# One ViT layer on one core: the lanes of the low waves change from wave-then-row to row-then-wave

## The chip, the core and the metric

The kernel runs on one core of a Trainium2 chip. A core has five engines with queues of their own: TensorE (PE, with weight loads shown apart as PEld), VectorE (DVE), ScalarE (ACT), GpSimd (POOL) and SyncE (SP), and 16 DMA engines that move data between HBM and the core's 128-partition memory. The time is the device time of the whole program in microseconds (us).

## The reference, cut to what matters

The program tokenizes 16 images of 1024 patches, then does one layer of attention and a small mixture of experts. What matters here is what happens to the keys of the attention: every element `x` of the 256 x 1024 keys of an image is replaced by a Fourier sum of 256 frequencies.

```
def kan_transform(x, kan_a, kan_b):
    freqs = jnp.arange(1, NUM_FUNCTIONS + 1, dtype=x.dtype)      # 1..256
    def body(acc, fab):
        f, af, bf = fab
        return (acc + af * jnp.sin(f * x) + bf * jnp.cos(f * x), None)
    out, _ = jax.lax.scan(body, jnp.zeros_like(x), (freqs, kan_a, kan_b))
    return out
...
k = kan_transform(k, kan_a, kan_b)
dots = jnp.einsum('bhqd,bhkd->bhqk', q, k) * scale
attn = jax.nn.softmax(dots, axis=-1)
```

## The kernel before

A frequency from 1 to 256 is written as one of 16 steps 16 w + 8.5 (w from 0 to 15; the program calls these waves *low*) plus or minus one of 8 offsets v + 0.5 (*high*). By the addition theorems the sum over all frequencies of one key row becomes sines of the 16 low waves, mixed by TensorE with the coefficients, times sines of the 8 high waves, summed by TensorE.

**Where the waves come from.** `keys` computes the keys of an image as turns (the angle as a 32-bit integer) and stores them from GpSimd to a buffer in HBM, `ud`, of shape [64, 2, 4, 2, 1024]: 64 blocks of four key rows, the angle once with a quarter turn added and once without (`f`), four rows (`e`), and every row twice (`i`), 1024 tokens. A row of 1024 integers has 4 KB.

**Groups.** Eight key rows are a group; an image has 32 groups (`NG`), the 16 images have 512. A group needs three tiles `w` of 128 partitions x 1024 (512 KB each), made by `load_waves`: two for the low waves (`j` = 0 and 1, line L709, one DMA of 512 KB each) and one for the high waves (`j` = 2, line L713, two DMAs of 256 KB, each for 64 partitions). All are broadcasts: a row of `ud` lands in many partitions, and each partition is then one (row, wave) pair. There are 12 buffers for `w` (`NW`).

**What is done with a tile `w`.** `turn_waves` (L728, GpSimd) multiplies it in place by the wave number of each partition, taken from the constant `lane`, so that the integers wrap round to the angle wanted. `sines` (L740, ScalarE) takes the sine. `mix` (L746, TensorE) multiplies the two low tiles by the coefficients `coef` into the PSUM tile `kan`; a column of `coef` sums over the partitions of one row. `times_fast` (L756, VectorE) multiplies `kan` by the high tile into `prod`, and `add_up` (L771, TensorE) sums that into `red`.

**Order.** The work is written out by hand in rounds: 130 rounds, of which 128 have four groups (eight low loads and four pairs of high loads). A round has four groups of waves first, then one attention step (`score` L817, `exponential` L827, `weigh` L835), and between them pieces of the other work (tokens, layer norms, queries, keys of the next image, experts), which `piece` picks by their due times. All loads of `w` go through SP's queue together with the loads of queries (`q<-qd`, L804) and keys (`k<-kd`, L792) and the stores of queries (L420) and keys (L784). GpSimd's queue holds the wave multiplications, the layer norm `hn` (L307), the stores of `ud` (L387) and the loads of the image (`x`, L286), in order.

In the kernel before, partition p of a low tile holds wave p // 8 of row p % 8: the eight rows (copy `i` = 0 of each) are written 16 times one below the other.

Of the kernel before, what the change touches and what calls it, by code (L numbers as in the profile page):

```python
# [22 lines left out]
N = 1024  # L23
# [32 lines left out]
def plain_path(ctx: ExitStack, tc: tile.TileContext, a: dict, out: bass.AP, verdict: bass.AP):  # L56
# [8 lines left out]
    nc = tc.nc  # L65
# [63 lines left out]
    for i in range(4):  # L129
        nc.sync.dma_start(out=biases[ds((NE + 1) * i, NE), 0, :], in_=a["eb3"])  # L130
        nc.sync.dma_start(
            out=biases[ds((NE + 1) * i + NE, 1), 0, :], in_=a["sb3"].unsqueeze(0)
# [13 lines left out]
    lane = const.tile([P, 2], INT, tag="lane", name="lane")  # L146
# [547 lines left out]
    def load_waves(n=NW):  # L694

        for _ in range(n):
            if ptr["load"] == min(3 * total, ptr["used"] + NW):
                return
            i = ptr["load"]
            g, j = divmod(i, 3)  # L700
            b, g = divmod(g, NG)
            st = images.get(b)
            if st is None or st.get(("rows", g // (NG // 2)), 0) < 2:
                return
            w = wp.tile([P, N], INT, tag="w", name="w")
            ud = st["ud"]
            if j < 2:
                src = ud[2 * g + j, :, :, 0, :].rearrange("f e n -> (f e) n")
                nc.sync.dma_start(out=w, in_=src.unsqueeze(0).to_broadcast([16, 8, N]))  # L709
            else:  # L710
                for s in range(2):
                    src = ud[2 * g + s].rearrange("f e i n -> (f e i) n")
                    nc.sync.dma_start(  # L713
                        out=w[ts(s, 64), :],
                        in_=src.unsqueeze(1).to_broadcast([16, 4, N]),
                    )
            w_tiles[i] = w
            ptr["load"] += 1
# [158 lines left out]
    feed(1, first_norm(0, 0), keys(0, 0))  # L877
    finish()
    load_waves()
    turn_waves(NW - 3)  # L880
    for ch in chains:
        ch["due"] = 0

    with tc.manual_schedule():
        for rd in range(B * RI + 2):
            now["round"] = rd
            b, rr = divmod(rd, RI)
# [21 lines left out]
            if attends:  # L909
                i, st = p % NPAIR, images[p // NPAIR]  # L910
# [5 lines left out]
            for n, g in enumerate(groups):  # L916
                sines(g)
                if n < 3:
                    turn_waves(1)
                if n == 0:  # L920
                    piece("sin")
                mix(g)
                if n > 0:
                    times_fast(groups[n - 1])
                    add_up(groups[n - 1])
                    if n != 2:
                        load_waves(3)
                    piece("sin")
# [3 lines left out]
            for n in range(0, NT, 2):  # L932
                if attends:
                    q4 = bands_of_queries[att]
                    score(q4, n)
                    exponential(n)
                    if n == 0:
                        piece(EXP)
                    score(q4, n + 1)
                    exponential(n + 1)  # L940
                if n == 0 and groups:
                    add_up(groups[-1])
                if n == 2 and groups and groups[-1] % 8 == 7:
                    finish_keys(groups[-1] // 8)
                if attends and n > 0:
                    weigh(p, n - 2)
                    weigh(p, n - 1)
                if n in (0, 4):
                    load_waves(3)
                if n == 2 and 0 <= att + 1 < 2 * NPAIR * B:  # L950
                    stack_queries(att + 1)
                turn_waves(2 if n < 6 else 3)
                piece(EXP)
                if n > 0 or not attends:
                    piece(EXP)
# [616 lines left out]
def _kan_layout(kan_a, kan_b):  # L1572

    a, b = kan_a.reshape(16, 16), kan_b.reshape(16, 16)
    a_hi, b_hi = a[:, 8:], b[:, 8:]
    a_lo, b_lo = a[:, 7::-1], b[:, 7::-1]
    first = np.block([[b_hi, a_hi], [a_hi, b_lo]])
    second = np.block([[b_lo, a_lo], [a_lo, b_hi]])
    outs = []
    for blk in (first, second):
        o = np.zeros((2, 32, 4, 16, 8), blk.dtype)
        for half in range(2):
            for e in range(4):  # L1590
                o[half, :, e, :, 4 * half + e] = blk
        outs.append(o.reshape(2, 128, 128))
    return outs
# [22 lines left out]
def _kan_tiles(kan_a, kan_b):  # L1616

    outs = []
    for blk in _kan_layout(kan_a, kan_b):
        b = blk[0].reshape(2, 16, 4, 2, 8, 8)[:, :, 0, :, :, 0].transpose(1, 0, 2, 3)
        o = np.zeros((16, 2, 4, 2, 4, 8), b.dtype)
        for e in range(4):
            o[:, :, e, :, e, :] = b
        outs.append(o.reshape(128, 64))
    return outs


def _waves():

    lane = np.arange(128)
    return np.stack([32 * (lane // 8) + 17, 2 * (lane % 8) + 1], 1).astype(np.int32)


def _pack():
# [63 lines left out]
```

## Time and profile before

| | |
|---|---|
| time, median of 4 runs | 5494.17 us (5474.49 to 5499.47) |
| the profiled execution: time, span | 5501.68 us, 5499.8 us |
| TensorE busy, share of the span | 4981.7 us, 91% |
| ScalarE, GpSimd, VectorE busy | 3154.2 us (57%), 3627.9 us (66%), 2382.9 us (43%) |
| granted TensorE clock, mean | 0.960 |
| bytes moved by the DMA engines | 1148.57 MB, mean 209 GB/s |
| loads of low waves (L709) | 1024 of 512 KB |
| loads of high waves (L713) | 1024 of 256 KB |

An engine's idle time costs only where it is on the path that sets the end. The profile names for each wait what ended it. The chain of the work that ended last is followed back only over the end of the program here, so the bound of the loop is read from the waits of each engine.

### The profile page before, as it was taken

Reading aid. Unit: us, or ns where it says so; the run is one execution under the profiler, and the core shown is the slowest. Engines: PE = TensorE matmul, PEld = TensorE weight load, DVE = VectorE, ACT = ScalarE, POOL = GpSimd, SP = SyncE. Lnnn points to the kernel's source line nnn. Section 1 sums busy time; section 2 is a strip of 40 time slices with the busy share of each in tenths; the row PEclk is TensorE's granted clock in tenths of the full one; section 3 lists DMA queues with packets and bytes.
Section 4 is the critical chain, followed back from the end, with each engine's and each line's share of the span. In section 5 each row is a group of like instructions: output and inputs, shape, how many; then the busy total and the mean of one; then the engine's idle time right before and its main releaser. Section 6 shows DMA issues by size and latency. Waiting matters only on the chain. (4 is left out here: it accounts for less than half of the span.)

```text
span 5499.8 us, 57562 instructions
## 1 busy us (share of the span) xinstructions
PE 4981.7 (91%) x18625; PEld 2130.0 (39%) x18625; DVE 2382.9 (43%) x3596; ACT 3154.2 (57%) x3517; POOL 3627.9 (66%) x2284
## 2 busy tenths in 40 slices
PE   6889899898999989999899998989999899998987
PEld 2324344343443434334343443434434343343334
DVE  2344435444443443444454344444434434444432
ACT  2556556555655655565565565556556555655652
POOL 6677857667576666757667576675766667576651
PEclk8999999999999999999999999999999999999998
DMA  7989988887887888888888888979879888888960
GB/s 205 225 239 221 234 214 198 224 217 208 220 221 204 209 220 214 230 204 199 220 215 229 210 199 219 216 213 220 225 201 214 212 215 231 202 199 219 217 159 14
DMA packets 360729, 1148.57 MB, mean 209 GB/s; under 512 B 53308, under 2 KB 57316, under 8 KB 352228
## 3 DMA queue, kind: packets, MB, share of 16 engines
q1 hardware_dynamic: 323044, 1010.57, 75.2%
q0 software_dynamic: 37376, 134.24, 7.4%
q8 instruction: 151, 2.47, 0.2%
q14 instruction: 158, 1.29, 0.1%
HBM read 993.61 MB, written 150.99 MB: 208 GB/s over the span
## 5 line engine op out<-in xcount | busy, mean ns | idle before, releaser
L728 POOL TENSOR_TENSOR w<-w,lane 128x1024 int32<-128x1024 int32 x1536 | 2885.8, 1908 | 1020.8 <-DMA w<-ud 798.5
L740 ACT ACTIVATE w<-w 128x1024 f32<-128x1024 int32 x1536 | 1497.7, 1046 | 327.2 <-POOL w L728 325.6
L827 ACT ACTIVATE es<-sT 128x1024 f32<-128x1024 f32 x1024 | 1036.8, 1023 | 705.4 <-PE sT L817 517.4
L746 PE MATMUL kan<-w,coef 128*64 128x512 f32 x4096 | 1191.1, 635 | 85.6 <-ACT w L740 85.5
L835 PE MATMUL av<-es,v 128*64 128x512 f32 x4096 | 1018.2, 620 | 2.1 <-DVE rc L859 2.1
L756 DVE TENSOR_TENSOR prod<-kan,w 128x1024 f32<-128x1024 f32 x512 | 626.2, 1223 | 780.3 <-PE red L771 664.9
L817 PE MATMUL sT<-q,k 128*128 128x512 f32 x2048 | 729.7, 468 | 65.3 <-ACT es L827 33.6
L771 PE MATMUL red<-prod,pack 128*64 128x512 f32 x2048 | 587.2, 632 | 208.1 <-DVE prod L756 207.5
L852 DVE RECIPROCAL rc<-av 128x512 f32<-128x512 f32 x128 | 429.5, 3356 | 781.0 <-PE av L835 780.7
L746 PEld LDWEIGHTS kan<-w,coef 128*64 128x64 f32 x4096 | 324.7, 143 | 836.6 <-issue 455.2
L827 ACT ACT_TABLE_LOAD x126 | 161.7, 1283 | 648.0 <-PE sT L817 647.9
L817 PEld LDWEIGHTS sT<-q,k 128*128 128x128 f32 x2048 | 367.3, 192 | 370.5 <-issue 162.1
L835 PEld LDWEIGHTS av<-es,v 128*64 128x64 f32 x4096 | 260.0, 140 | 515.7 <-issue 491.7
L286 POOL DMA_DIRECT2D x<-in_xT x128 | 110.6, 864 | 438.6 <-PE tok L209 303.2
L209 PE MATMUL tok<-wt,x 128*128 128x256 f32 x1536 | 377.1, 397 | 18.9 <-DMA x<-in_xT 18.9
L209 PEld LDWEIGHTS tok<-wt,x 128*128 128x128 f32 x1536 | 290.9, 196 | 159.2 <-issue 107.4
L771 PEld LDWEIGHTS red<-prod,pack 128*64 128x64 f32 x2048 | 137.0, 141 | 524.8 <-DVE prod L756 339.8
L307 POOL TENSOR_SCALAR hn<-h,mv,rstd 128x256 f32<-128x256 f32 x256 | 311.4, 1250 | 2.1 <-PE s2p L209 0.3
L209 PE MATMUL e1p<-hT,w1e 128*128 128x512 f32 x496 | 245.9, 619 | 0.9 <-ACT s L621 0.5
L346 DVE TENSOR_TENSOR h<-tok,tokb 128x256 f32<-128x256 f32 x128 | 54.1, 422 | 431.9 <-PE tok L209 431.9
L682 POOL DMA_DIRECT2D out<-h x32 | 26.5, 829 | 272.5 <-DVE h L680 228.2
L213 PE MATMUL lnT<-ident,hn 128*128 128x128 f32 x512 | 104.2, 325 | 106.8 <-POOL hn L307 102.1
(113 smaller groups left out, 4127.4 us busy)
## 6 DMA issues: line engine op xcount, KB each, us to landing
w<-ud SPq DMA_DIRECT2D x1024, 512.0 KB
w<-ud SPq DMA_DIRECT2D x1024, 256.0 KB
q<-qd SPq DMA_DIRECT2D x512, 128.0 KB
k<-kd SPq DMA_DIRECT2D x128, 512.0 KB
x<-in_xT POOLq DMA_DIRECT2D x128, 384.0 KB, 9.8
ud<-ui POOLq DMA_DIRECT2D x64, 512.0 KB, 9.9
ud<-u POOLq DMA_DIRECT2D x64, 512.0 KB, 8.2
qd<-qhi SPq DMA_DIRECT2D x64, 256.0 KB
```

What stands on the lines that cost most here:

```text
L209: nc.tensor.matmul(out=out, lhsT=lhsT, rhs=rhs, start=start, stop=stop)
L286: nc.gpsimd.dma_start(out=t, in_=xT[b, :, ts(j, XT)].rearrange("(c p) n -> p c n", p=P))
L307: nc.gpsimd.tensor_scalar(hn[:, t, :], h[:, t, :], mv[:, t, 0:1], rstd[:, t : t + 1], ALU.subtract, ALU.mult,)
L728: nc.gpsimd.tensor_tensor(w, w, f.to_broadcast([P, N]), ALU.mult)
L740: nc.scalar.activation(x, w, AF.Sin, scale=TURN * 2.0**-32)
L746: nc.tensor.matmul(out=ps[ts(j, 64), ts(blk, 512)], lhsT=coef, rhs=w_tiles[3 * g + j][:, ts(blk, 512)], start=True, stop=True,)
L756: nc.vector.tensor_mul(prod, kan.pop(g), w_tiles[3 * g + 2])
L771: nc.tensor.matmul(out=rows_of_pair[p][ts(blk, 64), :], lhsT=pack[:, ds(PACK0 - 8 * r, 64)], rhs=prod[:, ts(blk, 512)], start=(r == 0), st ...
L817: nc.tensor.matmul(out=ps[:, ts(s, 512)], lhsT=k4[:, s, ts(kc, P)], rhs=q4[:, s, :], start=True, stop=True,)
L827: nc.scalar.activation(es, scores.pop(kc), AF.Exp, scale=SCALE)
L835: nc.tensor.matmul(out=acc[0][ts(s, 64), :], lhsT=v[:, kc, p % NPAIR, ds(HD * s, 64)], rhs=es[:, ts(s, 512)], start=(kc == 0), stop=(kc == ...
L852: nc.vector.reciprocal(rc, av)
```

## The change

The low tiles' partitions are ordered by row, then by wave. `ud[2 * g + j]` has 16 rows of 4 KB in a row (eight different ones, each twice); each is now written to eight partitions one below the other, so that partition p holds row p // 16 and wave p % 16. The constants `lane` (from `_waves`) and `coef` (from `_kan_tiles`) are laid out to match. The sizes of all tiles and DMAs, and the order and number of instructions on every engine, stay as they were.

```
             if j < 2:
-                src = ud[2 * g + j, :, :, 0, :].rearrange("f e n -> (f e) n")
-                nc.sync.dma_start(out=w, in_=src.unsqueeze(0).to_broadcast([16, 8, N]))
+                src = ud[2 * g + j].rearrange("f e i n -> (f e i) n")
+                nc.sync.dma_start(out=w, in_=src.unsqueeze(1).to_broadcast([16, 8, N]))
...
-        b = blk[0].reshape(2, 16, 4, 2, 8, 8)[:, :, 0, :, :, 0].transpose(1, 0, 2, 3)
-        o = np.zeros((16, 2, 4, 2, 4, 8), b.dtype)
+        b = blk[0].reshape(2, 16, 4, 2, 8, 8)[:, :, 0, :, :, 0]
+        o = np.zeros((2, 4, 16, 2, 4, 8), b.dtype)
         for e in range(4):
-            o[:, :, e, :, e, :] = b
+            o[:, e, :, :, e, :] = b
...
-    return np.stack([32 * (lane // 8) + 17, 2 * (lane % 8) + 1], 1).astype(np.int32)
+    return np.stack([32 * (lane % 16) + 17, 2 * (lane % 8) + 1], 1).astype(np.int32)
```

## The prediction

> **What bounds the kernel now.** I read part 1 and the groups of the page first, then TensorE's waits, then GpSimd's, then three stretches by their DMA rate.
>
> The page, busy times and the costliest groups:
>
> ```profile
> PE 4981.7 (91%) x18625; PEld 2130.0 (39%) x18625; DVE 2382.9 (43%) x3596; ACT 3154.2 (57%) x3517; POOL 3627.9 (66%) x2284
> ...
> L728 POOL TENSOR_TENSOR w<-w,lane 128x1024 int32<-128x1024 int32 x1536 | 2885.8, 1908 | 1020.8 <-DMA w<-ud 798.5
> L740 ACT ACTIVATE w<-w 128x1024 f32<-128x1024 int32 x1536 | 1497.7, 1046 | 327.2 <-POOL w L728 325.6
> ```
>
> TensorE is the bound, with 518 us of idle time. GpSimd's wave multiplications wait 798.5 us for the loads of `w`, but most of that is slack. What reaches TensorE stands in its waits:
>
> ```profile
> PE red L771 <- DVE prod L756: 207.5, 91, 13.4
> PE lnT L213 <- POOL hn L307: 102.1, 69, 5.6
> PE kan L746 <- ACT w L740: 85.5, 98, 12.9
> ```
>
> These are late results, not late DMAs, so each has to be followed back. The timeline of one round shows how a late load arrives there:
>
> ```profile
> 2623.42 0.73 POOL L451 COPY v<-last 128x256 f32<-128x256 f32 x2
> 2630.49 1.89 POOL L728 TENSOR_TENSOR w<-w,lane 128x1024 int32<-128x1024 int32 x1 [6.34 <-DMA w<-ud]
> ...
> 2632.42 1.06 ACT L740 ACTIVATE w<-w 128x1024 f32<-128x1024 int32 x1 [1.79 <-POOL w L728]
> ...
> 2635.15 1.08 PE L771 MATMUL red<-prod,pack 128*64 128x512 f32 x4 [1.85 <-DVE prod L756]
> ```
>
> GpSimd sat 6.34 us for one load, ScalarE's sine came late, and TensorE lost 1.85 us. I followed every TensorE wait over 250 ns between 200 and 5300 us back from releaser to releaser: of 404 us, 159 us end at a load `w<-ud`, in 70 of the 128 rounds; 233 us end at no DMA (the reciprocal of 3.36 us ahead of `prod` above all). So loads of `w` hold some 159 us of the time, and the change touches two thirds of their bytes.
>
> How fast the DMAs run, by stretch (length, five engines' busy time, clock, DMA share, GB/s):
>
> ```profile
> 8.00:12.00 4.00, 0.99 (x2) 0.84 (x3) 0.00 (x0) 0.00 (x0) 0.00 (x0) 1.00 1.05 395
> ...
> 84.00:94.00 10.00, 5.70 (x16) 1.14 (x14) 3.74 (x4) 4.33 (x5) 8.58 (x5) 1.00 1.03 234
> ```
>
> In the first stretch the engines load weights and the image, 128 partitions at a time, each engine its own rows: 395 GB/s. In the second they load nothing but `w`: they are as busy, and move 234 GB/s. The question of this case is what costs the `w` loads that difference: that 16 engines read the same row (the change ends this), or something that the change leaves alone.
>
> **The change, part by part.** *Instructions.* The program has the same instructions in the same order on all engines. The 1024 loads of L709 keep 512 KB, 128 packets of 4 KB and an issue of 526 ns on SP; no wait is added, so nothing behind them in SP's queue moves. `lane` and the mixing constants are loaded once, in the same sizes. L728, L740 and L746 keep shapes and durations (1908, 1046 and 635 ns). All this costs nothing, and needs no cover. The bytes read from HBM are the same; 64 KB of them are distinct instead of 32 KB.
>
> *The loads themselves.* I take the price of one as the step from one landing to the next when the queue is full (landings by the semaphores, the DMA issued over 4 us before the one ahead of it landed). A low load after a low load: 2.24 us (484 cases). The two halves of a high tile, the same 512 KB: 1.00 + 1.17 = 2.17 us. High loads already have the new form on the reading side: each engine reads a row of its own, and repeats it, four times.
>
> Bounds for the new low load: at best its 128 packets take the 159 ns of the image loads and of the fastest tenth of its own, 128 x 159 / 16 = 1.27 us, a gain of 0.97 us. At worst it is as slow as the key loads `k<-kd`, own rows too, 512 KB in a step of 2.62 us: a loss of 0.38 us. I take 2.17 us, the high loads' step, a gain of 0.07 us, because it is the nearest row and because of the packets. In low loads (packet records of 667 complete sequences of one engine) the eight packets have medians of 274, 266, 254, 267, 274, 268, 252 and 268 ns; in high loads (1196) the four have 276, 266, 252 and 265. Whether an engine walks through shared rows or repeats its own, it goes through the same profile of four packets, and starts it again in the middle of a low load where no DMA ends. Four packets are four partitions; the reading side has nothing in common between the two. That says the writing side sets the pace, and the change does not touch it if an engine's eight partitions stay the same eight.
>
> [...]
>
> *On the path.* A round has eight low loads: 8 x 0.07 = 0.56 us. In the 70 rounds whose wait leads back to a load this is 39 us; half of a round's low loads land after the wait or ahead of an idle queue, so I count half, **20 us**. In the other 58 rounds the loads have slack and 0.07 us does nothing. Where a wait shrinks, the reciprocal and `prod` on VectorE are late next, so the 233 us stay. TensorE's half-clock time (445 us in the clock records) follows its waits; these shrink and do not vanish, so I count nothing for it.
>
> Sum: 5501.7 - 20 = 5481.7 us for the profiled execution, which lay 7.5 us above the median of the runs; from the median, **5474 us**. A difference under 0.3%, 16 us, is about what a measurement of this kernel cannot tell from none.
>
> **The rivals.** *Reading the same row is the cost.* Then a low load falls toward 1.3 us, the 159 us of waits go, and with them their share of the half-clock loss (445 / 2 = 222 us, times 159/468 of the loop's idle time, 76 us). Of 235 us I take 60%, since other waits come forward: -140 us, 5350 us (5260 to 5420). For it: 395 against 234 GB/s; and the load of `tokb`, one 1 KB row read by all engines, had packets of 152 ns on average, where the weight loads around it had a median of 46. Against it: `bout`, of the same form, had 46 ns; the first low load into an idle queue has its second and third packets at 159 ns with all engines on the same rows; and the high loads.
>
> [...]
>
> *It does not do what it says.* If an engine's eight partitions are not eight in a row, two engines share each row; or the rows do not matter at all. Then the step stays at 2.24 us and the time within 16 us of 5494.
>
> **How the numbers follow.** Forecast (step 2.15 to 2.22 us, 5450 to 5490 us): 0.40, of which 0.27 faster and 0.13 same. Shared rows were the cost: 0.14, faster. Nothing: 0.21, of which 0.19 same, 0.01 on each side. Into step: 0.25, of which 0.23 slower and 0.02 same. Together faster 0.42, same 0.34, slower 0.24. The range goes from 5400 us (it leaves out most of the shared-row case, 0.11) to 5545 us (it leaves out the upper half of the slower case, under 0.09).
>
> **What would show it.** Right: the stretch of nothing but `w` loads after 84 us at 235 to 245 GB/s, the median low packet at 262 to 272 ns with its restart after four packets, GpSimd's wait for `w<-ud` at 740 to 800 us. Shared rows: that stretch over 300 GB/s, packets near 159 ns, GpSimd's wait under 500 us and TensorE idle under 400 us. [...] The prediction is wrong if the packets change by more than 10 ns either way, or if they do not and the time moves by more than 30 us: then the path is not what I followed.

## The result, and the profile after

The kernel after takes 5490.66 us (median of 44 runs), the kernel before 5485.64 us (70 runs, those shown above among them). The ratio is 1.0007, with a 95% interval of 0.9998 to 1.0016: between 1 us less and 9 us more. The change makes no difference that counts, and the 20 us that were forecast are not there. The profiled execution after has a span of 5496.0 us (before: 5499.8) and the same mean clock of 0.960.

The page after, busy times and the two groups behind the loads (busy time and mean ns of one, then the idle time ahead of them and what ended most of it):

```profile
PE 4980.1 (91%) x18625; PEld 2132.0 (39%) x18625; DVE 2385.9 (43%) x3596; ACT 3153.8 (57%) x3517; POOL 3628.4 (66%) x2284
...
L728 POOL TENSOR_TENSOR w<-w,lane 128x1024 int32<-128x1024 int32 x1536 | 2886.5, 1908 | 1027.6 <-DMA w<-ud 725.2
L740 ACT ACTIVATE w<-w 128x1024 f32<-128x1024 int32 x1536 | 1497.6, 1046 | 338.0 <-POOL w L728 336.3
```

TensorE's waits after (us in total, times, longest):

```profile
PE red L771 <- DVE prod L756: 206.0, 89, 11.6
PE lnT L213 <- POOL hn L307: 104.5, 71, 5.6
PE kan L746 <- ACT w L740: 79.4, 97, 11.7
```

The two stretches by their DMA rate, after (length, five engines' busy time, clock, DMA share, GB/s):

```profile
8.00:12.00 4.00, 1.22 (x3) 1.04 (x4) 0.00 (x0) 0.00 (x0) 0.00 (x0) 1.00 1.05 395
84.00:94.00 10.00, 8.09 (x19) 1.80 (x18) 2.51 (x3) 4.89 (x5) 8.79 (x5) 0.68 1.04 238
```

Every line stands within some us of its counterpart. Only one looks like a gain: GpSimd's wait for `w<-ud` fell from 798.5 to 725.2 us, and no time came of it. The price of a load by landings did not move: a low load after a low load takes 2.244 us (471 cases; 2.24 before), and the two halves of a high tile 1.03 + 1.19 us (1.00 + 1.17). These steps, like all steps below, are means; single steps of low loads lie mostly between 1.4 and 3.0 us, which leaves a standard error of 0.03 us on the mean. The eight packets of a low load have medians of 280, 272, 256, 287, 284, 275, 254 and 281 ns, 2 to 20 ns above those before, and most of them above the 262 to 272 ns of the forecast. But the packets of the high loads, which the change leaves alone, rose by 7 to 15 ns as well (286, 276, 259 and 280), so this looks like a difference between two profiles rather than the change's.

### The profile page after: what moved, and what is told of

It reads as the page before. It is cut to its first block, busy times and chain, and to the rows that moved or that the text cites. A ratio compares the mean times of both kernels' runs of the same rounds, so it can differ in the third digit from the quotient of the medians.

```text
span 5496.0 us, 57562 instructions
## 1 busy us (share of the span) xinstructions
PE 4980.1 (91%) x18625; PEld 2132.0 (39%) x18625; DVE 2385.9 (43%) x3596; ACT 3153.8 (57%) x3517; POOL 3628.4 (66%) x2284
## 5 line engine op out<-in xcount | busy, mean ns | idle before, releaser
L728 POOL TENSOR_TENSOR w<-w,lane 128x1024 int32<-128x1024 int32 x1536 | 2886.5, 1908 | 1027.6 <-DMA w<-ud 725.2
L740 ACT ACTIVATE w<-w 128x1024 f32<-128x1024 int32 x1536 | 1497.6, 1046 | 338.0 <-POOL w L728 336.3
L771 PE MATMUL red<-prod,pack 128*64 128x512 f32 x2048 | 584.8, 628 | 206.7 <-DVE prod L756 206.0
```

Source lines behind the costliest of these rows:

```text
L728: nc.gpsimd.tensor_tensor(w, w, f.to_broadcast([P, N]), ALU.mult)
L740: nc.scalar.activation(x, w, AF.Sin, scale=TURN * 2.0**-32)
L771: nc.tensor.matmul(out=rows_of_pair[p][ts(blk, 64), :], lhsT=pack[:, ds(PACK0 - 8 * r, 64)], rhs=prod[:, ts(blk, 512)], start=(r == 0), st ...
```

## The experiments

Two questions were open: what sets the rate of a `w` load, if not the rows that it reads, and whether that rate is on the path at all. All edits are on the kernel after unless it says otherwise; ratios are to the kernel before, run on the same chip. An added or removed line shifts the line numbers of the kernels quoted below by a few.

**One row for all.** Each low load reads one row of 4 KB 128 times.

```
-                nc.sync.dma_start(out=w, in_=src.unsqueeze(1).to_broadcast([16, 8, N]))
+                nc.sync.dma_start(out=w, in_=src[0:1, :].to_broadcast([P, N]))
```

> The changed kernel, but every low load broadcasts one single row of ud to all 128 partitions (source a plain list of 128 repeats instead of 16 rows times 8 repeats); the sums of the keys are therefore not the reference's. All 16 engines now read the same 4 KB all the time: the most sharing there can be. Theory W (the writing side and the way the transfer is cut up for the engines set the pace, reading does not): sharing is harmless, the low loads are no slower than 2.24 us a step; and if cutting a plain list of 128 gives the engines other partitions than cutting 16 times 8, they reach the rate of the weight loads, a step near 1.35 us, packets near 159 to 200 ns, and the time falls by 100 to 200 us. Theory R (reading few rows is the cost, and both forms of the case read too few): this is the slowest of all, a step over 2.5 us and a time 50 to 200 us above the kernel before.

Measured: 5487.39 us, 1.0011 (0.9995 to 1.0027). The step of a low load fell to 1.98 us (432 cases), its packets to a median of 159 ns, and the stretch of `w` loads rose from 238 to 332 GB/s:

```profile
84.00:94.00 10.00, 8.43 (x20) 1.70 (x18) 2.51 (x3) 5.52 (x6) 9.57 (x6) 0.76 1.03 332
```

Sixteen engines on one row is the fastest form so far: reading shared rows is not the cost. And a load that is 0.26 us shorter, 1024 times, changed nothing in the time: the 100 to 200 us that were expected of faster loads did not come.

**128 rows, as a plain list and as 16 blocks of eight.** Both read rows at 128 different addresses and broadcast nothing; they differ in whether the source is one dimension of 128 rows (the first edit) or two, of 16 and 8 (the second).

```
-                src = ud[2 * g + j].rearrange("f e i n -> (f e i) n")
-                nc.sync.dma_start(out=w, in_=src.unsqueeze(1).to_broadcast([16, 8, N]))
+                first = 8 * (g // 4)
+                src = ud[first : first + 8].rearrange("b f e i n -> (b f e i) n")
+                nc.sync.dma_start(out=w, in_=src)
...
+                half = 32 * (g // 16)
+                src = ud[half + j : half + 32 : 2, :, :, 0, :].rearrange("b f e n -> b (f e) n")
+                nc.sync.dma_start(out=w, in_=src)
```

> The changed kernel, but every low load takes 128 neighbouring rows of 4 KB of ud, one for each partition, nothing repeated (a plain list of 128 on both sides); the sums of the keys are not the reference's. Theory W: as the single-row kernel, a step near 1.35 us if a plain list is cut up like the weight loads, 5300 to 5400 us; the stretch of nothing but w loads after 84 us goes from 238 to over 300 GB/s. Theory R: fast as well, since 128 different rows are read. So this kernel alone does not part the two; it tells how much time there is in faster low loads.

> The changed kernel, but every low load takes 128 different rows of ud, nothing repeated, as 16 blocks (128 KB apart) of 8 rows (8 KB apart), a source that cannot be written as one list of 128; the sums of the keys are not the reference's. Theory W: the cut is that of the case, 16 times 8, so the step stays at 2.2 to 2.3 us, packets near 270 ns, and the time within 16 us of the kernel before, although no row is read twice. Theory R: as fast as the 128 neighbouring rows, a step near 1.35 us and 100 to 200 us less.

Measured: the list has 159 ns packets and a step of 1.91 us; 16 x 8 has packets of 249 to 267 ns and a step of 2.229 us, as slow as the kernel after although no address is read twice. The same stretch, first of the list, then of 16 x 8:

```profile
84.00:94.00 10.00, 7.39 (x24) 1.71 (x23) 3.74 (x4) 5.96 (x6) 10.00 (x7) 0.96 1.03 325
```

```profile
84.00:94.00 10.00, 6.79 (x18) 1.71 (x18) 3.05 (x4) 4.38 (x5) 8.79 (x5) 0.90 1.03 241
```

So the form of the source sets the rate, 325 to 332 GB/s for a list of 128 and 234 to 241 for 16 x 8, whichever rows it names. The times go the other way: the list 5510.5 us, 1.0044 (1.0022 to 1.0066), a little slower than before; 16 x 8 5472.21 us, 0.9983 (0.9967 to 1.0).

What parts the two rates the traces do not show. They have two levels, 159 ns a packet for the list against 249 to 287 for 16 x 8, but their packet records name neither rows nor partitions: which engine read or wrote where is not shown.

**The high tile by one DMA.** The two loads of 16 rows, four lanes each, become one of 32 rows; the lanes hold the same waves as before. It was made on the kernel after and on the kernel before, and both were timed twice.

```
-                for s in range(2):
-                    src = ud[2 * g + s].rearrange("f e i n -> (f e i) n")
-                    nc.sync.dma_start(
-                        out=w[ts(s, 64), :],
-                        in_=src.unsqueeze(1).to_broadcast([16, 4, N]),
-                    )
+                src = ud[2 * g : 2 * g + 2].rearrange("s f e i n -> (s f e i) n")
+                nc.sync.dma_start(out=w, in_=src.unsqueeze(1).to_broadcast([32, 4, N]))
```

> The changed kernel with the high tile loaded by one DMA of 512 KB (32 rows, each to four neighbouring partitions) instead of two of 256 KB for 64 partitions each; the result is the same. 512 issues of SP less, and no half of the partitions is written alone. Theory W: what matters is which partitions are written together; 32 times 4 may be cut differently from 16 times 8. If cut in eights like the low loads, a step of 2.1 to 2.3 us for the tile and a time within 30 us of before; if cut in fours, near 1.4 us and up to 100 us less. Theory R: reading is as it was (32 rows repeated four times), so a step of 2.17 us and a time within 16 us, but for the saved issues.

> The kernel before, low loads in wave-then-row order, with the high tile loaded by one DMA of 512 KB as in the earlier run. Theory W (the order of the rows read does not matter) wants the same time as that run, 0.9963 of before, within 0.2%; if the row order mattered beside it, the two would differ by more.

> The kernel after with the high tile of a group by one DMA of 32 rows, four lanes each, in place of two DMAs of 16 rows: timed again, in more rounds and on the same chip as the kernel before with the same edit. Theory P (faster loads only move the wait to VectorE's chain, so a little is left to gain): 0.995 to 0.999 of before, both versions alike within 0.2%, since the rows that are read do not matter. Theory O (the row order matters once the high tile is one DMA): this one stays at 0.996 and the other at 0.9985 or more, a difference of over 10 us.

> The kernel before with the high tile by one DMA of 32 rows, four lanes each. Theory P (the rows that are read do not matter): within 0.2% of the kernel after with the same edit, on the same chip, 0.995 to 0.999 of before; the low step at 2.14 to 2.15 us and the high tile at 1.92 to 1.93 us in both. Theory O (the row order matters here): 0.9985 or more, over 10 us behind the other.

Measured: on the kernel after 5462.99 us, 0.9963 (0.995 to 0.9975), and again 5468.07 us, 0.9969 (0.9955 to 0.9984). On the kernel before 5470.78 us, 0.9987 (0.9972 to 1.0001), and again 5469.28 us, 0.9972 (0.9957 to 0.9987). Side by side on one chip the two differ by 1 us: the row order does not matter here either, and the 0.0024 that lay between them the first time did not come again. Over the four ratios the edit gives 0.1 to 0.4%, and these are the fastest versions that compute the whole reference. The high tile takes 1.93 us in place of 1.03 + 1.19, the low load 2.14 us, and SP issues 512 DMAs fewer; which of these gives the gain was not taken apart.

**All three tiles as lists.** The fastest loads of these experiments: each tile of a group from 128 neighbouring rows.

```
-            if j < 2:
...
+            first = 8 * (g // 4)
+            src = ud[first : first + 8].rearrange("b f e i n -> (b f e i) n")
+            nc.sync.dma_start(out=w, in_=src)
```

> The changed kernel with all three tiles of a group, the high one too, loaded each by one DMA from 128 neighbouring rows, nothing repeated; the sums of the keys are not the reference's. All loads of w are now cut as a plain list. Theory P (TensorE does not wait for the loads: its waits are set by VectorE's queue, above all the reciprocal and the operations behind it, and by the clock windows, so the time hardly follows the rate of the loads): the stretch after 84 us goes to 370 GB/s or more, the wait of GpSimd for loads falls below 450 us, and the time is within 0.6% of the kernel before, no faster than 5460 us. Theory F (the path of the prediction: waits lead back to the loads in 70 of 128 rounds): 100 to 200 us faster.

Measured: a step of 1.56 us, the stretch at 399 GB/s, the DMA engines busy on SP's queue for 56.0% of the span where it was 76.0%, and a time of 5554.18 us, 1.013 (1.0104 to 1.0156): slower, and outside both expectations. GpSimd waits 605.3 us for its loads in place of 725.2. TensorE waits less for the sines and more for VectorE:

```profile
PE red L764 <- DVE prod L749: 265.4, 104, 7.6
PE lnT L213 <- POOL hn L307: 100.9, 68, 5.6
PE kan L739 <- ACT w L733: 63.9, 86, 12.2
```

VectorE has the same instructions, but was busy for 2501.9 us, 116 us more than in the kernel after. With the low loads alone as lists it was 2437.1, with one row 2399.4: more than the 2385.9 of the kernel after in each of these runs. One small operation, the subtraction in line 473 ahead of the experts' softmax, accounts for all of it and more: its 32 executions come to 176 us here and to 27 us in the kernel after. Line 473 in this kernel, minimum, median and maximum in ns:

```profile
L473 DVE TENSOR_TENSOR gp<-g,gm x32: 175/1058/11282, 493.3 to 5514.5; 128x16 f32<-128x16 f32 x32
```

**The same, with that operation on GpSimd.**

```
-            nc.vector.tensor_sub(e, x, over_experts(m))
+            nc.gpsimd.tensor_tensor(e, x, over_experts(m), ALU.subtract)
```

> The kernel in which each of the three tiles of a group comes from 128 neighbouring rows by one DMA (other weights than the reference's, the same sizes), with one more edit: the subtraction of the maximum in the two softmaxes over the experts (line 473) is made by GpSimd, not by VectorE. Theory G (that kernel was slow because VectorE's queue stood some 10 us an image at this small operation, held behind GpSimd's wave multiplications): VectorE's queue stands no longer, the period of an image falls below 341 us, and the time falls from 5554 us by at least the 100 us and more that VectorE stood there, or as far as the rest of VectorE's chain lets it: 5440 to 5490 us. Theory L (the loop goes with the steps of the tensor clock, 341.3 us an image, and the standing is slack): the period stays at 341.3 us and the time within 0.4% of 5554. Between them, a GpSimd that takes the operation only after its queued multiplications makes VectorE wait for it as long as before: 5540 to 5560 with the wait now named as one for GpSimd.

Measured: 5616.2 us, 1.0245 (1.0229 to 1.0262), 62 us more and outside every expectation. VectorE's busy time fell only to 2454.3 us: other small operations took up to 1.93 us (`g`, L496; 0.149 us at its shortest) and 1.19 us (`gp`, L480; 0.174 us), and GpSimd now sat idle for VectorE's maximum, which stands just ahead of the moved operation:

```profile
L473 POOL TENSOR_TENSOR gp<-g,gm x32: 214/215/220, 492.7 to 5568.1; 128x16 f32<-128x16 f32 x32
...
  DVE gm L471: 303.4, 61
```

The edit put a new wait of 303.4 us into GpSimd's queue, so it does not tell whether the long operation is what makes the faster loads slower. That stays open: the 116 us on VectorE have the size for it, no more. TensorE shows only where the time went. Against the kernel after, in the profiled executions (spans of 5558.4 and 5496.0 us), it was idle some 25 us longer in the kernel with all lists, and busy 38 us longer with the same instructions (5018.0 against 4980.1 us), at a granted clock of 0.952 in place of 0.960.

**Slower loads.** Every third low load is followed by one more DMA of 320 KB into a tile that nothing reads, two in a round.

```
+    more = pool("more", 1)
...
+                if j == 0 and i // 3 % 2 == 0:
+                    again = more.tile([P, 640], INT, tag="again", name="again")
+                    nc.sync.dma_start(
+                        out=again,
+                        in_=src[:, 0:640].unsqueeze(1).to_broadcast([16, 8, 640]),
+                    )
```

> The changed kernel with two more loads a round, of the same cut as a low load (128 partitions from 16 rows, 320 KB, packets of 2.5 KB), into a tile that nobody reads: an estimated 1.4 us each by the step of 2.24 us for 512 KB, 2.8 us a round, 360 us of DMA time in all. Theory P: the loads have slack, and the time grows by less than 40 us. Theory F, with the prediction's rule (half of 70 rounds pays): 2.8 x 35 = 98 us more; if every round pays, 360 us.

Measured: 5632.8 us, 1.0269 (1.0242 to 1.0296), 154 us above the median of before on the same chip (147 by the ratio). GpSimd's wait for its loads rose to 1138.2 us, and TensorE's for the sines and for `hn` to 101.3 and 149.9 us. The 256 added DMAs would take some 360 us by themselves (256 x 320/512 of a 2.24 us step); the forecast's way of counting gave 98 us. So slower loads are hidden in part, some 200 of the 360 us, and not as far as either expectation said.

**A shorter VectorE chain.** The reciprocal ahead of `aT` becomes a copy.

```
-        nc.vector.reciprocal(rc, av)
+        nc.vector.tensor_copy(rc, av)
```

> The changed kernel with the reciprocal of the softmax sums on VectorE (3.36 us, 128 times) replaced by a copy of the same tile (about 0.7 us); the attention is therefore multiplied by the sums instead of divided. The loads are untouched. Theory P: the waits of red for prod, 206 us in the changed kernel, fall by half or more, and the time by 80 to 250 us. Theory F: loads arrive as before, so at most the waits without a load on their chain go, and the round then waits for loads: under 60 us.

Measured: 5347.85 us, 0.9747 (0.9719 to 0.9774), 131 us below the median of before on the same chip (139 by the ratio). TensorE's wait for `prod` went from 206.0 to 66.9 us, and its wait for the sines up to 107.3:

```profile
PE lnT L213 <- POOL hn L307: 117.5, 73, 6.4
PE kan L746 <- ACT w L740: 107.3, 112, 12.7
PE red L771 <- DVE prod L756: 66.9, 36, 14.4
```

**Both together.** The copy, and one row for all low loads.

> Two earlier edits together, on the kernel after: VectorE's reciprocal (line 852) is replaced by a copy, so that the attention is multiplied and not divided by its sums, and every low load reads one and the same row by a list of 128 (the weights of 127 in 128 rows are other than the reference's). Alone the first gave 0.9747 of before and the second 1.0011. Theory P (VectorE's chain covers the loads, so that faster ones gain nothing): with 131 us of that chain gone the loads have come nearer to the end (GpSimd waits 898 us for them in place of 725), so a part of the 186 us or so by which one row shortens the low loads now shows: 0.955 to 0.971, 5240 to 5325 us. Theory U (the loads are covered by something other than VectorE's chain, so its length does not decide): no gain here either, 0.972 to 0.978 as without the faster loads.

Measured: 5298.14 us, 0.965 (0.9624 to 0.9677). One row, worth nothing by itself, is now worth about 50 us (0.9747 less 0.965, of 5486 us; from the two intervals some 30 to 75). The waits have changed places again:

```profile
PE red L771 <- DVE prod L756: 116.6, 42, 8.4
PE lnT L213 <- POOL hn L307: 101.5, 68, 5.6
PE kan L746 <- ACT w L740: 65.5, 92, 11.0
```

With VectorE's chain shorter, faster loads take TensorE's wait for the sines from 107.3 to 65.5 us, and GpSimd's for the loads from 898.5 to 671.1. What a faster load is worth depends on the length of VectorE's chain: nothing with the reciprocal, about 50 us without it. So VectorE's chain covers the loads, at least in part. How much of the zero was cover is not shown, because faster loads also bring a cost: VectorE's busy time rose with one row in both pairs (2385.9 to 2399.4 us, 2087.8 to 2132.8), and without the copy the granted clock was 0.957 in place of 0.960.

## Why the prediction was wrong in its step, and right in its range

**What held.** The instructions: same counts, L728 at 1908 and L740 at 1046 ns, VectorE 2385.9 against 2382.9 us busy. So did half of the reason drawn from the packets, that the rows which are read do not set the pace. One row, the plain list and 16 x 8 show it: the rate goes with the form of the transfer and not with the rows. That it is the writing side which sets the pace fits, but no run shows which partitions an engine writes. GpSimd's wait for its loads fell a little further than the forecast said (725.2 us, not 740 to 800), which only shows how little that wait says of the time. The time lies in the range, but by the rival that had 0.21 ("or the rows do not matter at all": a step of 2.24 us, within 16 us), not by the step that the forecast took. A range from 1.6% below the time of before to 1.1% above it would have held almost any small effect, so that it held this one says nothing for the mechanism.

**The step that failed first: "I take 2.17 us, the high loads' step".** It measured 2.244 us. The 0.07 us between low and high loads were not the price of reading shared rows. With standard errors of 0.03 us on the low step and 0.02 on the sum of the high ones they were hardly a difference at all: after the change the same two stand at 2.244 and 2.22 us. (The 2.62 us for the key loads, the bound at worst, is a median beside these means; the mean of the key loads is 3.00 us.) The argument from the packets, followed to its end, gave a gain of zero, and zero should have been the forecast.

**The step that would have failed next: "so loads of `w` hold some 159 us of the time".** By the rule of the prediction one row would bring 0.26 us x 8 loads x 70 rounds / 2 = 73 us. It brought none: 1.0011, from 3 us less to 15 us more. The round that was quoted shows why, and the trace of the kernel before had it already:

```profile
2604.25 13.00 POOL L728 TENSOR_TENSOR w<-w,lane 128x1024 int32<-128x1024 int32 x7
...
2617.40 3.75 POOL L728 TENSOR_TENSOR w<-w,lane 128x1024 int32<-128x1024 int32 x2 [0.15 <-ACT hnT L322]
...
2627.85 3.36 DVE L852 RECIPROCAL rc<-av 128x512 f32<-128x512 f32 x1 [1.08 <-PE av L835]
...
2633.88 1.22 DVE L756 TENSOR_TENSOR prod<-kan,w 128x1024 f32<-128x1024 f32 x1
```

GpSimd's nine multiplications here are those of the round's first three groups, all done by 2621.15 us. The load that came late, for the multiplication at 2630.49, is the first tile of the fourth group. The `prod` for which TensorE lost 1.85 us is the first group's (counted in order, three multiplications and one `prod` to a group: groups 251 and 248). Its tiles had been multiplied by 2609.84 us, and what it waited for was VectorE, busy from the reciprocal on. The late load and the wait stand side by side in time, and do not belong together.

The same round after the change: GpSimd's wait, then VectorE's chain, then TensorE's waits:

```profile
2617.77 1.90 POOL L728 TENSOR_TENSOR w<-w,lane 128x1024 int32<-128x1024 int32 x1 [8.51 <-DMA w<-ud]
...
2613.14 3.36 DVE L852 RECIPROCAL rc<-av 128x512 f32<-128x512 f32 x1 [1.08 <-PE av L835]
2616.53 1.39 DVE L854 TENSOR_TENSOR aT<-av,rc 32x512 f32<-32x512 f32 x2
...
2619.18 1.22 DVE L756 TENSOR_TENSOR prod<-kan,w 128x1024 f32<-128x1024 f32 x1
...
2620.45 1.08 PE L771 MATMUL red<-prod,pack 128*64 128x512 f32 x4 [1.85 <-DVE prod L756]
2625.81 1.36 PE L771 MATMUL red<-prod,pack 128*64 128x512 f32 x4 [2.57 <-DVE prod L756]
```

And the same round with one row for all low loads:

```profile
2595.29 1.89 POOL L728 TENSOR_TENSOR w<-w,lane 128x1024 int32<-128x1024 int32 x1 [2.57 <-DMA w<-ud]
...
2596.61 3.36 DVE L852 RECIPROCAL rc<-av 128x512 f32<-128x512 f32 x1 [1.08 <-PE av L835]
2600.00 1.39 DVE L854 TENSOR_TENSOR aT<-av,rc 32x512 f32<-32x512 f32 x2
...
2602.65 1.22 DVE L756 TENSOR_TENSOR prod<-kan,w 128x1024 f32<-128x1024 f32 x1
...
2603.92 1.08 PE L771 MATMUL red<-prod,pack 128*64 128x512 f32 x4 [1.86 <-DVE prod L756]
2609.28 1.08 PE L771 MATMUL red<-prod,pack 128*64 128x512 f32 x4 [2.57 <-DVE prod L756]
```

GpSimd sat 6.34 us for that load before, 8.51 after and 2.57 with one row. TensorE lost 1.85, 1.85 and 1.86 us. From the reciprocal's start to `prod` it is 6.03 us before (2627.85 to 2633.88) and 6.04 in the other two (2613.14 to 2619.18, 2596.61 to 2602.65), without a gap: VectorE's queue brings `prod` when it does, and the load that the text named had nothing to do with it.

Over the whole kernel the sums fail in the same way. Counted as in the prediction, TensorE's waits that lead back to a load of `w`, and to no DMA, were 159 and 233 us before, 168 and 211 after, 80 and 313 with one row, 8 and 424 with all lists. The first sum nearly vanished, and the time did not fall. Such a sum depends on where a chain is allowed to end. If each chain ends as soon as it comes to work of TensorE itself, only 31 of the 404 us lead to a load before, 37 after, 3 with one row and 1 with all lists; if it goes on through TensorE's work, it comes to loads of earlier groups, and the sum grows past 100 us before the change. The prediction had the sentence that decides ("the reciprocal and `prod` on VectorE are late next, so the 233 us stay") and left it without a price. The copy in its place was worth 131 us, and only with it did faster loads show. The half-clock time, which the prediction counted at nothing, is a term too where the waits change. In the trace of the kernel before it goes with the waits: of the 3.413 us ahead of a piece at half clock TensorE was idle for 57% on average, ahead of one at full clock for 5% (pieces of 3.413 us, from 150 to 5300 us). Of the 142 us between the profiled executions of the kernel after and of the one with the copy, 50 are TensorE's busy time (4980.1 to 4930.6 us for the same matmuls, granted clock 0.960 to 0.967).

**The same rule for slower loads** was too low: 98 us counted, some 150 measured. Shorter loads gave nothing and longer ones cost less than half of their length.

**The rivals.** *Reading the same row is the cost* is excluded by one row (fastest) and by 16 x 8 (slow, with no row twice); so the long packets of `tokb` must have another cause, which no run shows. *Into step*, the slower case with a chance of 0.25, by which the range goes up to 5545 us, was the author's estimate: no run shows that engines wait for each other where they write, and it did not come. Step and stretch stand at 2.244 us and 238 GB/s. *The rows do not matter* is what the runs show.

## What to carry to other kernels

Look at the form of a DMA, not only at the rows that it reads: here the loads ran at 325 to 399 GB/s with plain lists of 128 rows and at 234 to 241 with 16 x 8, whether the rows were shared or not. Before a faster load is counted as time, look for the engine that is late next in the same round and price that one: here the faster load gave nothing, the slower one cost some 40% of what it added, and a gain appeared only with the other chain shortened too. Before a wait is put down to a load, check that the load's tile is one that the wait needs, and that the engine between them was not simply busy: in the quoted round neither held, and the sum of such waits did not bound what faster loads bring.

## What the runs showed of the hardware that was not expected

**A short VectorE operation as long as a row of GpSimd's.** With one row for all, the subtraction of 128 x 16 numbers, 174 ns at its shortest, took 11.26 us, and ended with GpSimd's eight multiplications in a row (the timelines of the two engines):

```profile
2649.42 14.89 POOL L728 TENSOR_TENSOR w<-w,lane 128x1024 int32<-128x1024 int32 x8
...
2653.09 11.26 DVE L473 TENSOR_TENSOR gp<-g,gm 128x16 f32<-128x16 f32 x1
```

Here it stood for the length of some six multiplications (14.89 us for eight, 1.86 us each): the last five or so of the eight started after it, and were done when it ended. It is no single case: all 45 VectorE operations in this run that took over 1.5 us longer than the shortest of their kind ended within 0.05 us of the end of a GpSimd operation. In the kernels before and after all such operations, 41 and 44, did the same. What makes them stand is not shown.

**Periods of 3.413 us.** With all lists, the first softmax of one image follows that of the one before at 341.33 us, ten images in a row and within 0.1 us; with the moved operation, at about 344.7 us. These are 100 and 101 times 3.413 us. With one row there are six of 98 times (334.5 us) in a row. In TensorE's clock records 90 of the 91 half-clock stretches of the kernel before, and 87 of the 88 of the kernel after, last 3.413 us or two to five times that. That a loop falls into step with this length is a reading of these periods, not tested. If it does, by the author's estimate a saving of less than 3.4 us an image (16 images, 55 us) can vanish in the next step, and some of what one row failed to gain may have gone there.
